# LayerNorm's small product on GpSimd, one more graph's rows by TensorE, and a new plan, in a two-layer graph attention kernel

## The chip, the core and the metric

The kernel runs on one core of a Trainium2 chip. The core has five engines with their own instruction streams: TensorE (PE in the profile; PEld is its weight load), VectorE (DVE), ScalarE (ACT), GpSimd (POOL) and SyncE (SP), which here only issues DMAs. Each engine takes its instructions strictly in the order in which they were written; they meet through semaphores. The metric is device time in microseconds, from the first instruction to the last with what lies around them.

## What is computed

There are 32 graphs of 512 nodes with 512 features in f32. Two layers, each with a LayerNorm, a ReLU and a residual:

```python
h = relu(layernorm(x));  x = x + L0(h, adj)
h = relu(layernorm(x));  x = x + L1(adj, h, W1, ..., W2, ...)

# L0: one head, on the features themselves
s = leaky_relu((h @ w_src)[:, :, None] + (h @ w_dst)[:, None, :] + b, 0.2)
attn = softmax(where(adj + eye == 0, -inf, s), axis=-1);  out = attn @ h

# L1: a layer of 4 heads with 256 features each (W1), ELU, a layer of 1 head (W2)
xl = x @ W;  e = leaky_relu(asrc[:, :, None] + adst[:, None, :], 0.2)
attn = softmax(where(mask, e, -1e9), axis=1);  out = attn^T @ xl + bias
```

## The kernel before

The body does not run a loop on the chip: all instructions of all 32 graphs are written out. The nodes of a graph are four tiles of 128 partitions. Each step is recorded with `op(engines, cost, emit, reads, writes, ...)`, where a cost is a pair or more of nanoseconds: how long the engine is occupied, how long after that the result is there, and for a DMA how long the transfer holds the DMA engines. `Plan.run` then makes one draft (`DRAFTS = 1`): a list scheduler in Python which, on the host and before anything runs, plays the program on five engines with these costs and writes the instructions out in the order that comes out. Of the steps that are ready, an engine takes the one with the lowest rank. The rank is the TensorE work recorded ahead of the step, less 1000 times the number that `LEADS` gives for the step's stage and engine (`"S0:DVE"`, `"first C:SP"`): a larger lead means earlier. The draft also decides which place a buffer gets. On the chip nothing of its times remains but each engine's order and each buffer's place; the instructions wait for data, not for times.

Two more of its rules matter. A step with `lock=True` on VectorE or GpSimd is not begun, in the draft, while a locked step of the other runs. And `self.turns` makes buffers of a kind be taken in the order in which they are first used, so the second graph's `x` cannot be loaded before the first's.

The stages of a graph, by the names that `LEADS` uses: LX loads x; S0 is the first LayerNorm, the ReLU, eight dot products with `ws_r` and `wd_r` on VectorE (line 464, VectorE's) and the scalar added to them (line 990); M0 loads and prepares the first mask; g (`guards`) computes a bound per row for the exponent, with line 796; e (`edge_weights`) makes the matrix of exponentials E: lines 840 (GpSimd), 845 (VectorE) and 852 (ScalarE), once for each of the four tiles. O0 is E times h on TensorE (line 864). I1 is the second LayerNorm, whose result is turned by DMA transposes (lines 701, 708, 717). P1 is the product with W1 (line 1178, a Strassen scheme with seven products). S10 to S13 and H0 to H3 are the four heads, P2 and O2 the last layer. O0 of graph b+1 and S0 of graph b+2 run inside the steps of graph b. For the first graphs this is not so: S0 and O0 of graph 0, I1 of graph 0 and S0 of graph 1 stand ahead of everything, and the stage name has "first " in front.

A vector of node values must be laid along the free dimension of all partitions for lines 796 and 845. There are two ways. `spread` does it on TensorE with four transposes of a broadcast column (line 634), straight into a PSUM bank. `in_lines` transposes once (line 748), copies to SBUF, writes to DRAM (line 754), and `row_of` reads it back to all partitions (line 765); `in_bank` copies it into PSUM (line 775). Before the change the first graph's layer-0 rows, and the last graph's rows of layer 2, go by `spread`, all others by `in_lines`. The guard's row goes by one of the same two ways (line 832 or 765).

LayerNorm (`layernorm`, from line 636): bn_stats and bn_aggr (lines 662 and 663), variance plus epsilon (line 665, VectorE), its power -1/2 on GpSimd (line 668), the negated product of mean and rstd on VectorE (line 673), and the ReLU with scale and bias on ScalarE (line 681). `STATS_BY_ACT` is False, so its other branch is not built.

The queues: SP issues every load of x, of the constants and of rows, the DMA transposes and the stores, in one order. GpSimd issues the adjacency loads (line 906), which turn int32 into bf16.

Of the kernel before, what the change touches and what calls it, by code (L numbers as in the profile page):

```python
# [13 lines left out]
ALU = mybir.AluOpType  # L14
# [29 lines left out]
class Plan:  # L44
# [8 lines left out]
        "first LXsoon:SP": 785.4, "first Csoon:SP": 105.6, "first C:SP": 575.5, "first Csoon:DVE": 111.1,  # L53
        "first Clater:DVE": -2168.5, "first Clater:SP": -124.3, "first S0:DVE": 54, "first S0:POOL": 54.1,
        "first S0:ACT": 54.2, "first S0M0:POOL": 40.3, "first S0M0:DVE": 37.9, "first S0M0:SP": 38,
        "first S0g:DVE": 220.7, "first S0g:PE": 221.7, "first S0e:PE": 116.5, "first S0e:ACT": 113.5,
        "first S0e:POOL": 117.7, "first S0e:DVE": 86.5, "first Clater:DVE+": -302.3, "first O0:PE": -14.2,
        "first O0:DVE": -14.9, "first Clater:PE": -622.9, "first I1:DVE": -27.8, "first I1:POOL": -32.7,
        "first I1:ACT": -34.4, "first I1:SP": 7.5, "first LX:SP": -173.2, "first S0:PE": 54.2, "first S0:ACT+": 54.8,
        "first S0:SP": 62.7, "first S0g:SP": 219.8, "first S0g:ACT": 226.9, "first S0g:ACT+": 259.3,  # L60
        "first S0e:SP": 132, "M1:POOL": -131.1, "M1:DVE": -58.6, "M1:SP": 497.4, "P1:POOL": -271.5, "P1:DVE+": -315.5,
        "P1:PE": -560.7, "P1:ACT+": -104.3, "P1:DVE": 81.7, "S10:ACT+": 15.8, "S10:PE": -3.7, "S10:SP": -5.3,
        "S10g:DVE": 26.8, "S10g:SP": 355, "S10g:ACT": 151.7, "S10g:PE": -41.6, "S10g:ACT+": 196.8, "S10e:SP": 150.1,
        "S10e:ACT": 84.1, "S10e:POOL": -13.9, "S10e:DVE": -29.6, "S11e:SP": 370.2, "S11e:ACT": -6.8,
        "S11e:POOL": -831.1, "S11e:DVE": -7.7, "O0:PE": -520.4, "O0:DVE": 9.8, "I1:DVE": -434.5, "I1:POOL": -437.7,
        "I1:ACT": -353.3, "I1:SP": -45.6, "LX:SP": 182.7, "S12:ACT+": -353.7, "S12:PE": -47.7, "S12:SP": 0.5,
        "S12g:DVE": -41.3, "S12g:SP": 287.8, "S12g:ACT": 166.3, "S12g:PE": -55.7, "S12g:ACT+": -10.5,
        "S12e:SP": 191.8, "S12e:ACT": -11.3, "S12e:POOL": 0, "S12e:DVE": 20.5, "H0:PE": -147.3, "H0:DVE": -16.3,
        "H0:ACT": -2, "H0:SP": 0, "S13e:SP": 153.5, "S13e:ACT": 138, "S13e:POOL": -420.2, "S13e:DVE": -145.4,
        "H1:PE": -1610.5, "H1:DVE": 44.9, "H1:ACT": 38.6, "H1:SP": -31.7, "H2:PE": -576, "H2:DVE": 407.8,  # L70
        "H2:ACT": 670.6, "H2:SP": 3.2, "H3:PE": 316.5, "H3:DVE": 329.5, "H3:ACT": 324.6, "H3:ACT+": 322.5,
        "S0:DVE": 48.1, "S0:POOL": -92, "S0:ACT": 170.3, "S0M0:POOL": -90, "S0M0:DVE": 97.6, "S0M0:SP": 153.4,
        "S0:PE": 282.3, "S0:ACT+": 102.1, "S0:SP": 553.1, "S0g:DVE": -202.3, "S0g:SP": 242.1, "S0g:ACT": 78.5,
        "S0g:PE": -64.8, "S0g:ACT+": 99.9, "S0e:SP": 151.7, "S0e:ACT": 344.9, "S0e:POOL": -14.4, "S0e:DVE": 19.6,
        "P2:POOL": 58.8, "P2:DVE+": 280.5, "P2:PE": -75.7, "P2:ACT+": -435.8, "P2:DVE": 25.5, "P2:SP": 338.6,
        "P2g:DVE": 172.1, "P2g:SP": 311.2, "P2g:ACT": 10.2, "P2g:PE": -5.8, "P2g:ACT+": 428.5, "P2e:SP": 238.7,
        "P2e:ACT": -58.2, "P2e:POOL": 63.9, "P2e:DVE": 117.7, "LB:SP": -2.9, "O2:PE": -586.8, "O2:DVE": 16.2,
        "O2:SP": 60.8, "last M1:POOL": 0.9, "last M1:DVE": -1.5, "last M1:SP": 22.2, "last P1:POOL": -254.4,
        "last P1:DVE+": 31.5, "last P1:PE": -56.6, "last P1:ACT+": -28.8, "last P1:DVE": -133.8,
        "last P2:POOL": -56.3, "last P2:DVE+": 1.4, "last P2:PE": 73.3, "last P2:ACT+": -39.5, "last P2:DVE": 13.5,  # L80
        "last P2:SP": -19.7, "last P2g:DVE": 147.5, "last P2g:SP": 95.3, "last P2g:ACT": 124.4, "last P2g:PE": 164.3,
        "last P2g:ACT+": 22.4, "last P2e:SP": 266.3, "last P2e:ACT": 228.3, "last P2e:POOL": 239.4,
        "last P2e:DVE": 228.3, "last S10:ACT+": 75.4, "last S10:PE": 27.1, "last S10:SP": 53.7, "last S10g:DVE": 71.7,
        "last S10g:SP": 27.3, "last S10g:ACT": 65.5, "last S10g:PE": 117, "last S10g:ACT+": 88.3, "last S10e:SP": 267,
        "last S10e:ACT": 276.6, "last S10e:POOL": 256.6, "last S10e:DVE": 253.5, "last S11e:SP": -323.5,
        "last S11e:ACT": -369.7, "last S11e:POOL": -375.4, "last S11e:DVE": -374.6, "last S12:ACT+": -443.3,
        "last S12:PE": -467.6, "last S12:SP": -468, "last S12g:DVE": -49.5, "last S12g:SP": -48.7,
        "last S12g:ACT": -62.1, "last S12g:PE": -46.6, "last S12g:ACT+": -85.4, "last S12e:SP": -67.5,
# [253 lines left out]
def kernel(  # L342
# [1015 lines left out]
    if B > 1:  # L1358
        load_x(1)
        layer0_scores(1)  # L1360
# [56 lines left out]
```

## Time and profile before

| quantity | value |
|---|---|
| median of 3 runs | 3603.31 us (3600.66 to 3608.34) |
| the profiled execution | 3606.86 us, its span 3604.9 us |
| granted TensorE clock, mean | 0.991 |
| VectorE busy | 2896.2 us (80%) |
| ScalarE busy | 1999.0 us (55%) |
| GpSimd busy | 1464.9 us (41%) |
| DMA traffic | 446.14 MB, mean 124 GB/s |
| chain of work that ended last | PE 76%, DVE 10%, DMA 7%, ACT 4% |

The profile is of one execution. Busy time of an engine is the sum over its instructions; the records of a matmul overlap their neighbours, so TensorE's busy time says that it had work in hand, not that it ran at its best. The chain of waits is followed back from the last instruction: what released it, what released that, and so on.

### The profile page before, as it was taken

To read this page: it belongs to the slowest core of one execution; us is meant where nothing else is said; L and a number is where in the kernel's file an instruction comes from. 1 tells how busy PE (TensorE), PEld (TensorE's weight loads), DVE (VectorE), ACT (ScalarE), POOL (GpSimd) and SP (SyncE) were. 2 spreads that over 40 slices of the span, in tenths; PEclk is the share of its full clock that TensorE was granted. 3 is DMA by queue.
4 is the path that set the end of the run, shared out by engine and by line. 5 is a ranking of instruction groups with operands and counts; after the bars stand their busy time and mean duration, and the time that the engine had idled before them with its cause. 6 is when DMAs were issued, how large, how long until landed. Compare 5 with 4: busy or idle time off the path is not lost.

```text
span 3604.9 us, 49251 instructions
## 1 busy us (share of the span) xinstructions
PE 3446.4 (96%) x15924; PEld 2946.9 (82%) x15924; DVE 2896.2 (80%) x7650; ACT 1999.0 (55%) x3356; POOL 1464.9 (41%) x1352
## 2 busy tenths in 40 slices
PE   3999999999999999999999999999999999999999
PEld 2778888888888888888888888888888888888888
DVE  7887788877888877888788888778888788887765
ACT  2565556555565555565555655555655555655553
POOL 2444435434344434354343444443444343543442
PEclk8999999999999999999999999999999999999999
DMA  6344445445454454554554554544545545545532
GB/s 169 112 117 124 110 117 142 128 129 130 93 141 126 130 129 108 119 139 128 131 128 97 141 132 129 129 123 100 148 120 130 131 108 125 137 130 132 128 81 80
DMA packets 664995, 446.14 MB, mean 124 GB/s; under 512 B 486072, under 2 KB 525216, under 8 KB 664736
## 3 DMA queue, kind: packets, MB, share of 16 engines
q1 hardware_dynamic: 630944, 409.43, 42.5%
q0 software_dynamic: 33792, 33.56, 6.3%
q8 instruction: 126, 2.06, 0.2%
q14 instruction: 133, 1.09, 0.1%
HBM read 290.72 MB, written 68.28 MB: 100 GB/s over the span
## 4 chain that ended last, share of the span: by engine, by line
PE 76%; DVE 10%; DMA 7%; ACT 4%; issue 1%; POOL 1%; SPq 0%; ACTq 0%; DVEq 0%; POOLq 0%
PE acc L864 38%; PE acc L1178 37%; DVE junk L464 3%; DMA row<-lines 3%; DVE junk L796 2%; ACT big L717 2%; ACT big L681 1%; DMA x<-in_x_dram 1%; DMA lines<-flat 1%; DMA out_dram<-x 1%; DVE ac L990 1%; ACT row L701 1%; PE acc L634 1%; PE acc L748 1%; DVE st L662 1%
## 5 line engine op out<-in xcount | busy, mean ns | idle before, releaser
L864 PE MATMUL acc<-big,big 128*128 128x257 f32 (+1 forms) x8192 | 1976.5, 383 | 39.4 <-ACT big L852 26.0
L864 PEld LDWEIGHTS acc<-big,big 128*128 128x128 f32 x8192 | 1539.0, 191 | 296.0 <-ACT big L852 36.6
L840 POOL TENSOR_TENSOR big<-m,big 128x512 f32<-128x512 bf16 x768 | 924.5, 1221 | 711.8 <-DMA big<-lines 381.2
L852 ACT ACTIVATE big<-big,ac 128x512 f32<-128x512 f32 x768 | 542.2, 720 | 291.0 <-DVE big L845 289.1
L845 DVE SCALAR_TENSOR_TENSOR big<-acc,ac,big 128x512 f32<-128x512 f32 x768 | 552.8, 740 | 92.4 <-POOL big L840 63.2
L689 ACT COPY big<-acc 128x258 f32<-128x258 f32 (+2 forms) x581 | 219.7, 384 | 619.3 <-PE acc L1178 614.6
L796 DVE CUSTOM_DVE_ANT_0 junk<-m,acc 128x512 bf16<-128x512 bf16 x768 | 522.8, 681 | 37.0 <-ACT acc L775 25.1
L1178 PE MATMUL acc<-w,big 128*128 128x258 f32 (+1 forms) x2048 | 519.2, 380 | 0.0
L1178 PE MATMUL acc<-w_T,sum 128*128 128x258 f32 (+1 forms) x2048 | 504.9, 381 | 3.0 <-POOL sum L1059 2.0
L1178 PEld LDWEIGHTS acc<-w_T,sum 128*128 128x128 f32 x2048 | 386.6, 190 | 63.2 <-POOL sum L1059 2.8
L1178 PEld LDWEIGHTS acc<-w,big 128*128 128x128 f32 x2048 | 385.5, 189 | 55.4
L446 POOL MEMSET big<- 128x4 f32 (+1 forms) x128 | 13.6, 107 | 950.3 <-PE acc L864 812.0
L1261 ACT ACTIVATE v<-acc,minus_one 128x256 f32<-128x256 f32 x512 | 231.4, 470 | 254.2 <-DVE acc L1254 245.9
L882 DVE SCALAR_TENSOR_TENSOR x<-acc,r,x 128x256 f32<-128x256 f32 x512 | 242.9, 481 | 109.7 <-PE acc L864 102.4
L1189 DVE TENSOR_TENSOR big<-acc,big 128x258 f32<-128x258 f32 (+1 forms) x576 | 242.3, 421 | 90.4 <-PE acc L1178 88.2
L1178 PE MATMUL acc<-w_T,big 128*128 128x258 f32 (+1 forms) x1024 | 263.7, 380 | 0.0
L1178 PE MATMUL acc<-w_-T,big 128*128 128x258 f32 (+1 forms) x1024 | 258.8, 380 | 0.0
L1178 PE MATMUL acc<-w,sum 128*128 128x258 f32 (+1 forms) x1024 | 252.7, 380 | 0.0
L1254 DVE SCALAR_TENSOR_TENSOR acc<-acc,r,b_r 128x256 f32<-128x256 f32 x512 | 242.3, 484 | 4.8
L1265 DVE SCALAR_TENSOR_TENSOR v<-v,acc 128x256 f32<-128x256 f32 x512 | 200.5, 409 | 36.0 <-ACT v L1261 35.7
L717 ACT COPY big<-v 128x1024 uint16<-128x1024 uint16 x192 | 222.0, 1156 | 2.5 <-DMA v<-row 2.1
L1178 PEld LDWEIGHTS acc<-w,sum 128*128 128x128 f32 x1024 | 194.1, 190 | 28.2
(89 smaller groups left out, 3340.1 us busy)
## 6 DMA issues: line engine op xcount, KB each, us to landing
big<-lines SPq DMA_DIRECT2D x380, 256.0 KB
row<-lines SPq DMA_DIRECT2D x190, 256.0 KB
x<-in_x_dram SPq DMA_DIRECT2D x32, 1024.0 KB
m<-in_adj_dram POOLq DMA_DIRECT2D x64, 512.0 KB, 5.9
spill<-x SPq DMA_DIRECT2D x32, 1024.0 KB
x<-spill SPq DMA_DIRECT2D x32, 1024.0 KB
out_dram<-x SPq DMA_DIRECT2D x30, 1024.0 KB
v<-row SPq DMA_TRANSPOSE x192
```

What stands on the lines that cost most here:

```text
L689: "ACT": (on_act_copied(n), lambda: nc.scalar.copy(dst_of(), src_of())),
L717: nc.scalar.copy(out.bitcast(U16).rearrange("p k t (n b) -> p k t n b", b=2), values_of().bitcast(U16).rearrange("p (b t k n) -> p k t n b ...
L796: lambda t=t, j=j, a_row=a_row: nc.vector.tensor_tensor_reduce(by_blocks(junk), mask_row(mask_max, t), by_blocks(a_row.at), 1.0, LOWEST, A ...
L840: lambda t=t: nc.gpsimd.tensor_sub(by_blocks(E.at[:, t, :]), mask_row(mask, t), by_blocks(g_at())),
L845: lambda t=t: nc.vector.scalar_tensor_tensor(E.at[:, t, :], c_row.at, ac.at[:, 4 + j, t : t + 1], E.at[:, t, :], op0=ALU.max, op1=ALU.add),
L852: lambda t=t: nc.scalar.activation(E.at[:, t, :], E.at[:, t, :], AF.Exp, bias=ac.at[:, 2 * j, t : t + 1]),
L864: lambda s=s: nc.tensor.matmul(acc.at[:, :n], E.at[:, s, node_block(t)], of(s), start=(s == 0), stop=(s == T - 1)),
L882: lambda acc=acc, r=r, f=f, t=t: nc.vector.scalar_tensor_tensor(X.at[:, t, f], acc.at[:, :HD], r.at, X.at[:, t, f], op0=ALU.mult, op1=ALU. ...
L1178: lambda k=k: nc.tensor.matmul(acc.at[:, :width], at[a](k // 2)[:, k % 2, node_block(r)], weight_of(w, k, c), start=(begin and k == 0), st ...
L1189: op("DVE", on_dve(width), lambda: nc.vector.tensor_add(place(), acc.at[:, :width], place()), acc(0) + token, token)
L1254: lambda acc=acc, r=r: nc.vector.scalar_tensor_tensor(acc.at[:, :F], acc.at[:, :F], r.at, b1_r[:, h * F : (h + 1) * F], op0=ALU.mult, op1= ...
L1261: lambda i=i, v=v, acc=acc: nc.scalar.activation(v.at[:, i, :], acc.at[:, :F], AF.Exp, bias=minus_one), acc(0), v(i),
```

## The change

Four edits.

1. `layernorm`: VectorE negates the mean (a new step, 128x4), and GpSimd, which has just made rstd, multiplies the two itself. VectorE's product after GpSimd goes.
2. `layer0_scores`: the rows of graph 1, like those of graph 0, go by `spread` (`b > 1` in place of `b`; flag 3 stands for both rows).
3. Costs of the draft: constant loads, the occupation of SP by a transposed mask, and the step of line 990, which is also locked now. The two small VectorE steps of LayerNorm get 60 more elements as cost, and GpSimd's power 1050 in place of 1000 ns.
4. All of `LEADS` is new, and x and S0 of graph 1 have a stage of their own, "second ".

```diff
     LEADS = {
-        "first LXsoon:SP": 785.4, "first Csoon:SP": 105.6, "first C:SP": 575.5, "first Csoon:DVE": 111.1,
-        "first Clater:DVE": -2168.5, "first Clater:SP": -124.3, "first S0:DVE": 54, "first S0:POOL": 54.1,
...
+        "first LXsoon:SP": -70.5, "first Csoon:SP": -73.5, "first C:SP": -177, "first Csoon:DVE": -9.2,
+        "first Clater:DVE": -132.1, "first Clater:SP": -583.1, "first S0:DVE": -115.7, "first S0:POOL": -129.1,
...
+        "first I1:ACT": -316.8, "first I1:SP": -13.3, "second LX:SP": -31.3, "second S0:DVE": 237.4,
...
         def fetch(n, place, src, token, when):
-            op("SP", by_dma(4 * P * n), lambda: nc.sync.dma_start(place(), src), (), token, when)
+            op("SP", (600.0, 2500.0, 4 * P * n / 190.0), lambda: nc.sync.dma_start(place(), src), (), token, when)
...
-            op("DVE", on_dve(T), lambda: nc.vector.tensor_scalar(ve.at, mv.at[:, :, 1], EPS, None, op0=ALU.add), mv(*ROW), ve(0))
-            mean_of, sign = (lambda: mv.at[:, :, 0]), -1.0
-        op(
-            "POOL", (1000.0, 1000.0), lambda: nc.gpsimd.tensor_tensor(rstd.at, ve.at, minus_half, ALU.pow),
+            op("DVE", on_dve(T + 60), lambda: nc.vector.tensor_scalar(ve.at, mv.at[:, :, 1], EPS, None, op0=ALU.add), mv(*ROW), ve(0))
+            op(
+                "DVE", on_dve(T + 60), lambda: nc.vector.tensor_scalar(minus_mean.at, mv.at[:, :, 0], -1.0, None, op0=ALU.mult),
+                mv(*ROW), minus_mean(0),
+            )
+        op(
+            "POOL", (1050.0, 1080.0), lambda: nc.gpsimd.tensor_tensor(rstd.at, ve.at, minus_half, ALU.pow),
             ve(0), rstd(0), lock=True,
         )
         op(
-            "DVE", on_dve(T),
-            lambda: nc.vector.scalar_tensor_tensor(nmr.at, mean_of(), sign, rstd.at, op0=ALU.mult, op1=ALU.mult),
-            mean(*ROW) + rstd(0), nmr(0),
+            "POOL", (150.0, 200.0), lambda: nc.gpsimd.tensor_tensor(nmr.at, minus_mean.at, rstd.at, ALU.mult),
+            minus_mean(0, *((0, t) for t in ROW)) + rstd(0), nmr(0), lock=True,
         )
...
-                "SP", by_turning(2 * P * N * (T if whole else 1)),
+                "SP", (6500.0 if len(adj_loads) < 3 else 1800.0, *by_turning(2 * P * N * (T if whole else 1))[1:]),
...
-            "DVE", on_dve(T), lambda: nc.vector.tensor_scalar(ac.at[:, 1, :], ac.at[:, 1, :], b0_r, None, op0=ALU.add),
-            c + W["w0"]("rest"), c,
+            "DVE", on_dve(T + 60), lambda: nc.vector.tensor_scalar(ac.at[:, 1, :], ac.at[:, 1, :], b0_r, None, op0=ALU.add),
+            c + W["w0"]("rest"), c, lock=True,
...
-        lines = in_lines(first(ac, 2), scores, 2) if b else None
-        L0[b] = (h0, edge_weights(scores, ac, lines, 0, guards(scores, ac, lines, 1, m0, 0 if b else 3), m0T))
+        lines = in_lines(first(ac, 2), scores, 2) if b > 1 else None
+        L0[b] = (h0, edge_weights(scores, ac, lines, 0, guards(scores, ac, lines, 1, m0, 0 if b > 1 else 3), m0T))
...
     if B > 1:
+        plan.stage = "second "
         load_x(1)
         layer0_scores(1)
+        plan.stage = "first "
```

## The prediction

> **What bounds the kernel now.** I read the page first, then the table by stretches, then TensorE's waits, then the order of instructions around the two largest.
>
> ```profile
> PE 3446.4 (96%) x15924; PEld 2946.9 (82%) x15924; DVE 2896.2 (80%) x7650; ACT 1999.0 (55%) x3356; POOL 1464.9 (41%) x1352
> PE   3999999999999999999999999999999999999999
> ```
>
> TensorE is busy 3446.4 of 3604.9 us; 158.5 us are open to a better order. The forty digits show one poor slice, the first. The table by stretches (PE busy second after the length; the column behind POOL is the granted clock) says how the 158.5 divide:
>
> ```profile
> 0.00:105.00 105.00, 44.28 (x157) 34.93 (x158) 77.22 (x253) 25.86 (x33) 21.94 (x29) 0.84 0.61 150
> 105.00:420.00 315.00, 296.14 (x1350) 251.47 (x1349) 259.13 (x708) 187.62 (x317) 136.34 (x124) 0.98 0.46 119
> 420.00:3300.00 2880.00, 2807.65 (x13023) 2403.01 (x13022) 2347.93 (x6131) 1630.08 (x2746) 1198.66 (x1102) 1.00 0.50 125
> 3300.00:3604.00 304.00, 298.36 (x1398) 257.49 (x1397) 211.95 (x561) 155.45 (x261) 107.94 (x99) 1.00 0.40 106
> ```
>
> Idle: 60.7 us up to the first graph's P1 (line 1178 begins at 105), 18.9 in the next 315, 72.4 in the even stretch (26 graphs of some 110 us, so 2.75 us each), 5.6 at the end. TensorE's waits name the causes:
>
> ```profile
> PE acc L748 <- DVE ac L990: 52.8, 28, 2.4
> PE acc L634 <- DVE junk L464: 30.6, 4, 27.1
> PE acc L864 <- ACT big L852: 26.0, 5, 11.7
> PE acc L748 <- DVE guard L814: 22.0, 13, 9.4
> ```
>
> So there are two places: the start (rows two and three, and 9.4 of row four) and one repeated wait of 52.8/28 = 1.89 us per graph.
>
> **The start, before.** Timeline of the three steps that hold it:
>
> ```profile
> 25.53 0.69 DVE L464 SCALAR_TENSOR_TENSOR junk<-big,ws_r 128x512 bf16<-128x512 f32 x1
> ...
> 62.88 0.27 PE L748 MATMUL acc<-ident,ac 128*8 128x128 f32 x1 [1.84 <-DVE x L882]
> ...
> 84.46 4.89 POOL L840 TENSOR_TENSOR big<-m,big 128x512 f32<-128x512 bf16 x4 [12.56 <-DMA big<-lines]
> ```
>
> Graph 0's x has landed at 6.32 (bn_stats starts) and its ReLU runs 11.33 to 14.26, but the dots begin at 25.53: `ws_r` was issued at 12.80, behind the attention vectors and W1, and was scaled at 23.85. The dots end at 31.91, E's first tile reaches TensorE at 47.21 (15.3 us later), O0 of graph 0 ends at 67.1. From there to P1 there are 38 us: bn_stats, the product on VectorE (L673 at 75.22, though GpSimd's power was done at 71.9: four L796 stood ahead of it), the ReLU, transposes, sums. Graph 1's x was issued at 30.56; its dots end at 62.21, and its E reaches TensorE at 88.44.
>
> **Part 1, order of loads.** The new ranks on SP put x of graph 0 first, then x of graph 1 (its lead -31.3 and some 22 us of recorded work give about 53, but it must wait its turn), then `ws_r`, `wd_r`, `b0_r` (73.5), and only then the vectors and W1 (177). At 300 GB/s (the DMA rate of 5 to 10 us), 1 MB of x and 0.5 MB of the two vectors are 5 us behind x of graph 0: landed about 12. Dots can begin at 12.5 in place of 25.5, 13 us earlier. All is not gained. "second S0:DVE" leads by 237.4, so graph 1's bn_stats (4 x 0.66, with aggregation 3.5) and dots (8 x 0.73 = 5.9) may go ahead of graph 0's: that is up to 9.4 us back. Bounds on graph 0's E: 13 and 3.6 us earlier; I take 8. W1 then lands some 5 us later than its 12.9 to 22, but nothing on TensorE needs it before P1. SP is held 5.83 us by the first transposed mask (issued 22.42); x of graph 1 and the vectors are past it now, only W1's remainder and the later constants stand behind.
>
> **Part 2, graph 1 by TensorE.** It removes two `in_lines` and three `row_of`: five DMAs. By the trace: end of L990 62.44 to the row in its bank 68.47 (row landed 67.88, ScalarE copy 0.59) = 6.0 us; graph 0 by `spread` takes from 32.14 to 33.05 = 0.9. Guard ready 76.31 to GpSimd's start 84.46 = 8.2; graph 0: 36.94 to 39.47 = 2.5. Together 10.8 us off graph 1's E. Twelve transposes of about 0.27 us (3.3 us) are added and two taken away; TensorE is empty there (3.94 us busy between 65 and 90), so they cost nothing; without that cover, 2.7 us. E of graph 1 arrives after x landed some 25 us earlier and this together well before 70.
>
> **Sum of the start.** What is late next is graph 0's path through O0 and I1 to P1. It moves by 8 us, and by the 3.3 us that L673 stood behind L796 at 75.22 (the product is now on GpSimd, not in VectorE's queue); O0 of graph 1 (17.1 us), which before filled the time from 88.44 to 105.55 and kept P1 from its data (the last L717 copy ends at 93.2), is done by then: up to 4 more. I take 14 us; bounds 3 and 25.
> The Trainium skill has a rule here ("TensorE: Matmul & The Clock Gate", why this matters for your kernels): avoid idle gaps over some 3 us, since the array falls back to half clock. The trace shows it: granted clock 0.50 from 75 to 90 and 0.55 from 90 to 95, so O0 of graph 1 lost about 3.5 us. The new start still has a gap before P1: by the rule a like loss stays, only on P1. By row and rule alike I book nothing back.
>
> **Part 3, LayerNorm.** 64 times. VectorE: one 128x4 step for another. L673 took a median 0.159 us and at most 1.234 (37.3 us over 53 in the even stretch); L665, the form of the new one, 0.16. If it escapes GpSimd it saves 53 x 0.54 = 29 us of VectorE, which has 19% to spare, so 0 on the time. GpSimd: the nearest rows are the memset of 128x4 (0.10 us) and the power of 128x4 (1.04); I take 0.15, nearer the memset since the power is the dear part: 64 x 0.15 = 10 us, bounds 6 and 66, on an engine idle 59%. Behind it in GpSimd's order stand L1059 and L840, whose readers would be 0.15 (at most 1.0) us later once in two LayerNorms' worth per graph. Nothing on TensorE in the even stretch waits for L673 or L681 by name. I book 0; from -5 to +10 us.
>
> **Part 4, the repeated wait.** One graph's order around it:
>
> ```profile
> 797.28 7.21 POOL L840 TENSOR_TENSOR big<-m,big 128x512 f32<-128x512 bf16 x5 [4.90 <-DMA big<-lines]
> ...
> 798.08 1.46 DVE L464 SCALAR_TENSOR_TENSOR junk<-big,ws_r 128x512 bf16<-128x512 f32 x1
> ...
> 799.59 1.52 DVE L464 SCALAR_TENSOR_TENSOR junk<-big,wd_r 128x512 bf16<-128x512 f32 x1
> ...
> 801.04 1.11 DVE L990 TENSOR_SCALAR ac<-ac,b_r 128x4 f32<-128x4 f32 x1
> ...
> 802.21 0.27 PE L748 MATMUL acc<-ident,ac 128*8 128x128 f32 x1 [2.40 <-DVE ac L990]
> ```
>
> Two dots take 1.46 and 1.52 in place of 0.69, and L990 1.11 in place of its free 0.22: all three lie beside GpSimd's L840. Behind the waiting transpose stand 62 matmuls, so each microsecond is TensorE's. The plan expected L990 to cost 0.07. The slip is 0.89 from L990 and 1.6 from the dots. The change prices L990 at 0.14 and keeps it, in the draft, off GpSimd. If the plan so places the transpose later by L990's excess, 28 x 0.89 = 25 us go.
> Against this speaks the skill's page "SBUF — State Buffer" (who interferes with whom): VectorE and GpSimd share a port pair as an exclusive lock, and whichever starts first keeps it for its whole instruction. A lock in a host's draft holds no engine: it works only where GpSimd really starts when the draft says. The dots were locked in the old draft too, and still were doubled. By L990's row the gain is 25 us, by this reading 0. I take half, 12; bounds -53 (the wait gone wholly) and 0.
>
> **Part 5, the rest of the plan.** Every lead is new, so every order in the even stretch is. No row shows what that does. TensorE's 2.75 idle us per graph bound the gain (72 us with part 4 in it). For the loss the nearest row is the wait above: one more transpose or matmul set 1.9 us too early, in each graph. I take 0. The end has 5.6 us idle in 304: -4 to +10, taken 0.
>
> **Sum.** -14 - 12 = -26 on the profiled 3606.9: 3581. This execution lay 3.6 us above the median of the runs, so **3577**.
>
> **Rivals.**
> - **The wait goes wholly.** The new order puts in_lines behind enough matmuls: -53 - 15 = -68, 3535. For it: the costs mended (L990, L673) are those that the trace shows mispriced. Against: the 1.6 us from the dots, which the prices do not touch.
> - **Nothing is left.** 14 us from the start, given back at 0.5 us per graph in the even stretch: 3603.
> - **A new wait per graph.** A transpose (L748) or product set too early behind a VectorE or GpSimd step that slips: 28 x 1.9 = +53, less 14: 3642. It decides from 0.5 us per graph on. For it: VectorE is 82% busy, a slip repeats in each graph since all graphs have one order, and L814 already makes such waits (22.0 us, 13 times). Against: the wait of L990 stands there already and the new prices are closer.
> - **The start does not move** because graph 1 ahead on VectorE eats it: 3591, inside the first case's range.
>
> **Chances.** The forecast 0.46 (its own range 3555 to 3596), wait gone 0.19, nothing left 0.09, a new wait 0.26. What can be told from no change is 0.2%, 7 us: faster 0.65, same 0.09, slower 0.26. The range runs from 3527 to 3630: it leaves out the deep end of the second case (0.04) and the larger half of the last (0.15).
>
> **What would show it.** Right: `ws_r` issued before 5 us and the first dots near 12 to 16; no line 748 or 754 before 100 us; P1's first matmul near 91 in place of 105; L990 near 0.2 us and its wait under 30 us in TensorE's list. Wrong: P1 later than 102; a wait with 28 entries under another name; L990 still at 1.1. GpSimd's new step over 0.5 us would move its 10 us to over 30. If TensorE's idle time between 420 and 3300 exceeds 86 us, the last rival has won.

## The result, and the profile after

The changed kernel takes 3590.05 us (median of 18 runs, 3585.65 to 3596.36); the kernel before, run beside it on the same chip, 3603.84 us (18 runs). The ratio is 0.9964, with a 95% interval of 0.9956 to 0.9972: 13.8 us faster where 26 were forecast. The direction was right, the size half.

Lines of the changed kernel are one higher than before from line 464 on, LayerNorm's own apart (464 is 465, 748 is 749, 990 is 991, 1178 is 1179); the new product of LayerNorm on GpSimd is line 674.

First the table by stretches of the changed kernel, with the columns and the stretches shown before:

```profile
0.00:105.00 105.00, 55.47 (x234) 46.68 (x235) 89.35 (x286) 37.97 (x52) 31.47 (x37) 0.90 0.67 153
105.00:420.00 315.00, 291.77 (x1319) 246.92 (x1318) 253.83 (x695) 176.84 (x296) 134.29 (x126) 0.96 0.46 117
420.00:3300.00 2880.00, 2813.79 (x13053) 2410.92 (x13052) 2332.47 (x6220) 1626.43 (x2679) 1218.66 (x1162) 1.00 0.51 126
```

TensorE's idle time in the first 105 us fell from 60.7 to 49.5 us, in the even stretch from 72.4 to 66.2, and rose from 18.9 to 23.2 between 105 and 420. Then TensorE's waits:

```profile
PE acc L749 <- DVE ac L991: 57.8, 29, 2.3
PE acc L635 <- DVE ac L991: 22.0, 1, 22.0
PE acc L865 <- ACT big L853: 15.3, 6, 11.1
```

The repeated wait, 52.8 us in 28 before, stands there as it was. The guard's wait under the transpose of line 748 (22.0 us in 13 before) is gone; at the start, where two graphs go by `spread` now, two single waits on guard steps stand under line 635 (10.3 and 9.3 us).

When did each kernel have the same share of TensorE's matmul records behind it? Worked out from the starts in both traces:

```
share of matmuls        1%     2%     3%     4%     5%    10%    40%    95%   99.9%
before, us            105.6  147.0  183.4  225.9  260.3  438.8 1500.7 3431.6 3597.2
after, us              77.5  123.0  162.2  219.1  253.7  428.9 1485.3 3416.2 3584.5
lead of the change     28.1   24.0   21.2    6.8    6.6    9.9   15.3   15.4   12.7
```

So the start won over 20 us, 14 of them were lost again in one place, the even stretch won about 9, the end lost 3. The place is seen in the stretch that holds the same 160 matmuls in each kernel, first before, then after:

```profile
183.00:226.00 43.00, 35.68 (x163) 30.32 (x163) 39.45 (x120) 25.74 (x43) 15.81 (x15) 0.92 0.47 117
```

```profile
162.00:219.00 57.00, 39.62 (x162) 30.98 (x161) 47.06 (x135) 28.86 (x45) 16.53 (x15) 0.85 0.43 93
```

57 us in place of 43, at a clock of 0.85 in place of 0.92. (From 3% to 4% of the matmuls it is 55 to 60 us in all fourteen later runs that keep the changed kernel's plan, so this is no chance of one execution.) Its largest wait is the first exponents of graph 2 (line 853), 11.1 us at 198.6, where the kernel before waited 7.3.

### The profile page after: what moved, and what is told of

Its sections match the earlier page's. It is cut to its first block, busy times and chain, and to the rows that moved or that the text cites. A ratio compares the mean times of both kernels' runs of the same rounds, so it can differ in the third digit from the quotient of the medians.

```text
span 3592.2 us, 49368 instructions
## 1 busy us (share of the span) xinstructions
PE 3445.8 (96%) x15934; PEld 2949.1 (82%) x15934; DVE 2877.7 (80%) x7726; ACT 1990.1 (55%) x3274; POOL 1488.4 (41%) x1419
## 4 chain that ended last, share of the span: by engine, by line
PE 79%; DVE 7%; DMA 6%; ACT 6%; issue 1%; POOL 0%; SPq 0%; ACTq 0%; DVEq 0%; POOLq 0%
PE acc L1179 40%; PE acc L865 37%; DVE junk L465 3%; DMA row<-lines 3%; ACT big L718 2%; ACT big L682 2%; DVE junk L797 2%; DMA v<-row 2%; DMA lines<-flat 1%; ACT row L702 1%; DVE ac L991 1%; PE acc L635 1%; PE acc L749 1%; DMA big<-lines 1%; ACT big L853 0%
## 5 line engine op out<-in xcount | busy, mean ns | idle before, releaser
L841 POOL TENSOR_TENSOR big<-m,big 128x512 f32<-128x512 bf16 x768 | 927.3, 1225 | 642.2 <-DMA big<-lines 357.7
L853 ACT ACTIVATE big<-big,ac 128x512 f32<-128x512 f32 x768 | 540.9, 720 | 217.0 <-DVE big L846 214.7
L690 ACT COPY big<-acc 128x258 f32<-128x258 f32 (+2 forms) x526 | 203.1, 387 | 746.9 <-PE acc L1179 721.3
L846 DVE SCALAR_TENSOR_TENSOR big<-acc,ac,big 128x512 f32<-128x512 f32 x768 | 551.6, 740 | 63.8 <-POOL big L841 52.1
L1060 POOL TENSOR_TENSOR sum<-big,big 128x512 f32<-128x512 f32 x31 | 39.0, 1260 | 466.3 <-ACT big L718 466.3
```

Source lines behind the costliest of these rows:

```text
L690: "ACT": (on_act_copied(n), lambda: nc.scalar.copy(dst_of(), src_of())),
L841: lambda t=t: nc.gpsimd.tensor_sub(by_blocks(E.at[:, t, :]), mask_row(mask, t), by_blocks(g_at())),
L846: lambda t=t: nc.vector.scalar_tensor_tensor(E.at[:, t, :], c_row.at, ac.at[:, 4 + j, t : t + 1], E.at[:, t, :], op0=ALU.max, op1=ALU.add),
L853: lambda t=t: nc.scalar.activation(E.at[:, t, :], E.at[:, t, :], AF.Exp, bias=ac.at[:, 2 * j, t : t + 1]),
```

## The experiments

Sixteen kernels were run, each beside the kernel before on the same chip. A planner that is asked anew may draw a whole new order, so most of them keep every engine's order and every buffer's place of the changed kernel and alter one thing; the two that are planned anew are marked. The kernel before lay at 3601 to 3605 us (medians) in these sessions, so a few us against the changed kernel's 3590 mean nothing. The diffs of those that move steps show the order of instructions on an engine.

### The repeated wait: first try

The first two take the place apart: the transpose set later, and the addition of line 991 on another engine.

```diff
 the S0 transpose of line 749, its copy and its DMA write, in the order of the draft
-start[i]
+start[i] + 2100.0
```

> The changed kernel's order kept, except that in S0 the transpose of line 749, its copy and its DMA to DRAM stand 2.1 us (some five matmuls) further back in their engines' orders. Theory A (TensorE is the bound and this wait is lost time, 57.8 us in 29 graphs): the wait under 10 us, the time 40 to 55 us lower, about 3540. Theory B (the wait is slack: the next step is late by the same amount, so another wait takes its place): the wait of line 749 gone, others up by as much, the time within 7 us of the changed kernel.

Measured: 3592.65 us, ratio 0.9975 [0.9965, 0.9985]: nothing gained. The wait on line 991 went, and an equal one came (lines here are 17 higher than in the changed kernel, so 882 is 865 and 708 is 691):

```profile
PE acc L882 <- DVE flat L708: 54.6, 30, 2.5
```

The matmul behind the moved transpose needs the PSUM bank that the transpose fills and VectorE's copy must empty first.

```diff
-nc.vector.tensor_scalar(ac.at[:, 1, :], ac.at[:, 1, :], b0_r, None, op0=ALU.add)
+nc.scalar.activation(ac.at[:, 1, :], ac.at[:, 1, :], AF.Identity, bias=b0_r)
```

> The changed kernel's order kept; the scalar of line 991 is added by ScalarE in place of VectorE, at the same place of the order. Theory A (line 991 takes 1.11 us only because GpSimd's line 841 runs beside it on what the two share; ScalarE does not share it): the step 0.2 to 0.3 us, the wait of line 749 shorter by 0.7 to 0.9 us per graph, 20 to 26 us off the time. Theory B (the two dots ahead are the delay, and a wait on another engine adds what is saved): under 8 us.

Measured: 3553.22 us, ratio 0.9866 [0.9850, 0.9882], 37 us under the changed kernel. On ScalarE the addition takes 0.30 us and is done before the last dot, so it leaves the path; what is left is the last dot:

```profile
PE acc L749 <- DVE r L1252: 30.0, 28, 1.5
```

That is 57.8 - 30.0 = 27.8 us less waiting. The rest of the 37 is clock, told at the end: 3.4 us at half clock between 420 and 3300 in place of 23.9, so some 10 us.

### LayerNorm, and VectorE's total

```diff
-"POOL", (150.0, 200.0), lambda: nc.gpsimd.tensor_tensor(nmr.at, minus_mean.at, rstd.at, ALU.mult)
+"POOL", (150.0, 200.0), lambda: nc.vector.tensor_tensor(nmr.at, minus_mean.at, rstd.at, ALU.mult)
```

> The changed kernel's order kept; LayerNorm's small product is made by VectorE again (the negated mean stays a step of its own), at the same place of the order. Theory A (the product is on no path that TensorE waits for, from I1 and S0 of the even graphs): within 7 us of the changed kernel. Theory B (GpSimd's own product is what the change gained): slower by 8 to 14 us, mostly in the first 260 us.

Measured: 3591.26 us, ratio 0.9972 [0.9962, 0.9981], no different from the changed kernel. On GpSimd line 674 takes a median of 0.216 us (at most 0.713), on VectorE 0.155 (at most 1.012). ScalarE's ReLU waits for the VectorE form 76.9 us in 33 entries, and TensorE notices none of it.

The next leaves out the 32 dots that VectorE makes for W2's score columns at the start (these columns are set to 0). It asks whether VectorE's sheer work there makes the hole at 170 to 200 us.

```diff
-dot(lo[:, 2:], flat(att[1])[:, i * D : i * D + W2 - 2], part[:, k, i : i + 1])
+nc.vector.memset(lo[:, i : i + 1], 0.0)
```

> The changed kernel's order kept, but the 32 dot products on VectorE that make the two score columns of W2 are left out (the columns are set to 0), some 16 us of VectorE in the first 105 us. Theory A (VectorE's work holds the first 200 us, and that is where the 21 to 28 us of lead at 80 to 180 us go): P1 of graph 0 begins at 82 as before or earlier, the hole of TensorE between 170 and 200 us shrinks, 8 to 16 us off the time. Theory B (that hole is the chain of DMAs and row loads of graph 1's first head): under 3 us off.

Measured: 3589.01 us, ratio 0.9969 [0.9956, 0.9981], and the wait for graph 2's first exponents is still 11.6 us, though VectorE is busy 80.60 us of the first 105 in place of 89.35. The total does not make the hole.

### The repeated wait: moving it about

```diff
 TensorE, in each graph
-L749 (S0's scores)
 L865 x5
+L749 (S0's scores)
```

> The changed kernel; every engine's order and every place kept, except that on TensorE up to five matmuls that stood behind the S0 transpose of line 749 now stand ahead of it (some 1.3 us and more of work). Theory A (the wait on line 991 is an order on TensorE alone: a transpose some 2 us too early, with other matmuls behind it that have their data): the wait on L991 falls from 57.8 us to under 15, TensorE idles 40 to 55 us less than in the changed kernel, the half-clock windows that follow the waits go too (up to 10 us), and the time is 3530 to 3550. Theory B (what stands behind is no readier, or it needs the transpose's PSUM bank, as in the run with the transpose postponed): an equal wait turns up under another name and the time stays within 10 us of 3590.

> Both edits together: line 991's addition on ScalarE (3553 alone) and up to four matmuls ahead of the S0 transpose of line 749. What is left of the wait with the addition on ScalarE is 30.0 us in 28 entries, 1.07 each, on the last dot. Theory A: it goes too, 20 to 28 us, so 3525 to 3533. Theory B: the matmuls put ahead leave the transpose's chain (transpose, copy, line write, row load, guard) too late for the exponents of that graph, and a wait on L853 or L814 takes its place: no faster than 3548.

Measured: 3593.39 us, ratio 0.9963 [0.9951, 0.9975], and with the addition on ScalarE 3554.66, ratio 0.9858 [0.9844, 0.9871]. Neither moves by more than 4 us from the kernel that it was made from. The first kernel's waits:

```profile
PE acc L865 <- ACT big L853: 65.5, 33, 11.5
```

The transpose no longer waits, and the matmuls behind it wait for exponents instead, about as long. Both stand behind the same dots in VectorE's queue: the transpose behind line 991, and L853 behind an L846 that VectorE reaches 2 us after it. Theory B held in each, with VectorE's queue as the thing behind it. The next two therefore move L846 forward too.

```diff
 VectorE, in each graph, on top of the last two
 L465 ws_r (tile 4)
+L846
 L465 wd_r (tile 4)
+L846
 L1252, L1255, L691, L1266 ...
-L846
-L846
```

> The version of 3555 (line 991 on ScalarE, up to four matmuls ahead of the S0 transpose) with two more moves in each graph: on VectorE the next two L846 stand on either side of S0's last dot instead of some 2 us behind it, and on ScalarE the first of their L853 stands ahead of three L1262. Theory A (what TensorE lacks at this place is VectorE's queue: the doubled dots delay whatever stands behind them, first the transpose, and when that is out of the way L846 and with it L853): the wait on L853, 50.0 us in 34, loses its 28 or so entries of 1.2 us, and the time is 3520 to 3532. Theory B (the chain behind S0's scores to the next layer-0 exponents is what binds, and it is as long as before): the wait turns up elsewhere and the time stays within 6 us of 3555.

> The same two moves on the version with line 991 left on VectorE and up to five matmuls ahead of the transpose (3593). There L853 is waited for 65.5 us in 33 entries, some 1.8 each. Theory A (VectorE's queue): with L846 in front, most of that goes, line 991 at its 1.1 us notwithstanding; what is left is the transpose, for which five matmuls are not cover enough by about 0.7 us: 3545 to 3565. Theory B (line 991 and its late transpose bind by themselves): above 3580.

Measured: with the addition on ScalarE 3553.39 us, ratio 0.9856 [0.9843, 0.9870], nothing gained; with it on VectorE 3565.63, ratio 0.9891 [0.9876, 0.9906], 28 us gained, just past the slow end of what theory A expected. In the first the long waits went (TensorE's idle time in the even stretch fell from 43.7 to 16.6 us), and yet no time was gained: the steps between two matmul starts show many small hold-ups instead, 283 of 0.235 to 0.6 us with 42 us over the usual 0.217, where there had been 52 with 6. TensorE's busy time hides them. What each of them waits for was not followed; it looks as if, whatever stands first in VectorE's queue, something behind it is late.

### The repeated wait: its cause

If VectorE's queue is it, then a microsecond taken from it anywhere ahead of the place must count, and line 991 can stay as it is. The next kernel halves four of the eight dots (scores of the first two tiles over 256 of 512 features, from graph 2 on).

```diff
-dot(h0.at[:, t, :D], w, ac.at[:, i, t : t + 1])
+n = D // 2 if b > 1 and t < 2 else D
+dot(h0.at[:, t, :n], w[:, :n], ac.at[:, i, t : t + 1])
```

> The changed kernel with every order kept; from the third graph on, the S0 dots of the first two tiles run over 256 of the 512 features (scores differ for these nodes): four steps of 0.42 us in place of 0.69, 1.1 us less on VectorE per graph, as much as line 991 takes, and ahead of it. Line 991 is left alone. Theory A (any microsecond taken from VectorE's queue at this place counts, whichever step gives it): the wait on L991 falls by about 1 us a graph, from 57.8 to under 35, and the time by 25 to 40, as with the addition on ScalarE: 3550 to 3565. Theory B (line 991's own collision with GpSimd sets the wait, and GpSimd's L841 starts when its row lands): dots that end sooner only lengthen nothing, line 991 still takes 1.1 and the wait stays over 45 us: above 3580.

Measured: 3520.28 us, ratio 0.9770 [0.9756, 0.9783]. Taking 1.1 us per graph gave 70 us, 2.3 per graph, and the wait on line 991 fell from 57.8 to 4.2 us. More came back than was taken out, since the dots now mostly end before GpSimd's L841 begins: of the last 28 graphs, all had dots of over 1 us in the changed kernel, and 10 have here.

```profile
PE acc L749 <- DVE ac L991: 4.2, 11, 1.0
```

So it was looked for where VectorE could save the time with nothing left out. Here is the place in the changed kernel, in the timeline of VectorE, of GpSimd, of SP and of TensorE:

```profile
785.14 0.43 DVE L691 COPY big<-acc 128x257 f32<-128x257 f32 x1 [1.25 <-PE acc L1179]
785.48 0.27 DVE L691 COPY flat<-acc 8x128 f32<-8x128 f32 x1
...
786.01 0.69 DVE L465 SCALAR_TENSOR_TENSOR junk<-big,ws_r 128x512 bf16<-128x512 f32 x1
...
790.62 1.46 DVE L465 SCALAR_TENSOR_TENSOR junk<-big,ws_r 128x512 bf16<-128x512 f32 x1
792.12 1.52 DVE L465 SCALAR_TENSOR_TENSOR junk<-big,wd_r 128x512 bf16<-128x512 f32 x1
793.58 1.11 DVE L991 TENSOR_SCALAR ac<-ac,b_r 128x4 f32<-128x4 f32 x1
```

```profile
790.16 5.74 POOL L841 TENSOR_TENSOR big<-m,big 128x512 f32<-128x512 bf16 x4 [4.89 <-DMA big<-lines]
```

```profile
785.77 0.30 SPq L755 DMA_DIRECT2D lines<-flat  x1
787.05 0.36 SPq L766 DMA_DIRECT2D big<-lines  x1
```

```profile
794.74 0.27 PE L749 MATMUL acc<-ident,ac 128*8 128x128 f32 x1 [2.05 <-DVE ac L991]
```

VectorE stands idle for 1.25 us behind a copy that waits for TensorE (the bracket of the first row), with all eight dots queued behind it, though the first tile has been ready since 784.7. At 790.16 its row releases GpSimd's L841; the last two dots run beside it, and each takes twice its time. The row has its origin in the same place: it is the guard's line, which the second copy (`flat`, 785.48) takes out of PSUM, and which SP then writes to DRAM (L755) and reads back (L766). The next kernel moves two dots, on VectorE alone:

```diff
 VectorE, in each graph
+L465 ws_r (tile 1)
+L465 wd_r (tile 1)
 L691, L691, L691, L784
-L465 ws_r (tile 1)
-L465 wd_r (tile 1)
 L465 ws_r (tile 2) ...
```

> The changed kernel; on VectorE alone, in each graph, the first two S0 dots (first tile, whose ReLU is done at 784.7 in the graph looked at) stand ahead of three copies of line 691 and line 784; the first copy waits for TensorE until 785.14, with VectorE idle for 1.25 us. Nothing is left out. Theory A (any microsecond of VectorE's queue ahead of the transpose counts): the dots end about 1.2 us sooner, most of them before GpSimd's L841 begins, the wait on L991 falls from 57.8 us to under 25, the half-clock windows go, and the time is 3520 to 3550. Theory B (the copies, now 1 us later, are wanted as urgently: the heads' scores go through them): a wait on L749 or L865 behind L691 of 1 us a graph takes its place, and the time is above 3575.

> The same order on VectorE, with line 991's addition on ScalarE (3553 alone, where 30.0 us in 28 entries are left on the last dot). Theory A: that wait goes too, and the time is 3515 to 3528, a few us under the run with line 991 on VectorE. Theory B: as for the other, above 3545.

Measured: 3526.42 us (3524.2 to 3529.6), ratio 0.9788 [0.9775, 0.9802], and with line 991 on ScalarE as well 3526.27, ratio 0.9785 [0.9771, 0.9798]. Two dots moved by four steps are worth 64 us, and the addition's engine is worth nothing any more. The same place in the first of the two:

```profile
771.80 0.69 DVE L465 SCALAR_TENSOR_TENSOR junk<-big,ws_r 128x512 bf16<-128x512 f32 x1 [0.83 <-ACT big L682]
...
773.49 0.27 DVE L691 COPY flat<-acc 8x128 f32<-8x128 f32 x1
...
777.81 0.69 DVE L465 SCALAR_TENSOR_TENSOR junk<-big,wd_r 128x512 bf16<-128x512 f32 x1
778.42 1.12 DVE L991 TENSOR_SCALAR ac<-ac,b_r 128x4 f32<-128x4 f32 x1
```

```profile
778.35 4.65 POOL L841 TENSOR_TENSOR big<-m,big 128x512 f32<-128x512 bf16 x4 [6.01 <-DMA big<-lines]
```

```profile
780.13 0.27 PE L749 MATMUL acc<-ident,ac 128*8 128x128 f32 x1
```

All dots take 0.69 us and end as L841 begins. Line 991 still takes 1.12, and nothing waits for it: the transpose has no bracket. In TensorE's list 1.0 us is left on line 991. A wait of the kind that theory B named has come, 0.36 us per graph where it said 1, and the even stretch is nearly full:

```profile
PE acc L749 <- DVE ac L691: 10.8, 30, 1.9
PE acc L749 <- DVE ac L991: 1.0, 1, 1.0
```

```profile
420.00:3300.00 2880.00, 2860.27 (x13341) 2461.89 (x13340) 2344.58 (x6380) 1670.51 (x2752) 1218.53 (x1187) 1.00 0.53 129
```

This version beats both kernels, by 77 and 64 us: 50 of the 64 are TensorE's idle time (146.4 us in the changed kernel, 96.3 here, each the span less PE's busy time), and some 12 the clock in the even stretch.

Why did the collision end? The 1.25 us that VectorE stood idle are not the reason. They shrink only to 0.83, in which it now waits for the first tile's ReLU. And in the run with five matmuls ahead of the transpose (3593) there is a graph in which VectorE does not idle at this place at all (the copy has no bracket), and the last two dots are doubled all the same:

```profile
788.55 0.43 DVE L691 COPY big<-acc 128x257 f32<-128x257 f32 x1
...
794.08 1.46 DVE L465 SCALAR_TENSOR_TENSOR junk<-big,ws_r 128x512 bf16<-128x512 f32 x1
...
795.58 1.53 DVE L465 SCALAR_TENSOR_TENSOR junk<-big,wd_r 128x512 bf16<-128x512 f32 x1
```

What counts is the order of the dots and the `flat` copy. Worked out from the traces for the last 28 graphs, L841 begins 4.4 to 5.5 us after the end of that copy in the changed kernel (median 4.4) and 4.4 to 5.1 us after it here (4.6): a copy that comes later starts GpSimd later. With eight whole dots behind the copy, the last ends 1.7 to 3.6 us after L841 has begun, in every graph; with six, from 0.4 before it to 0.4 after, and none is doubled. The kernel before has the same order here, and in all of its last 28 graphs the last dots are doubled too.

The move of the two dots thus did two things. Two dots fewer lie between the copy and L841; and the copy itself comes 0.9 us later behind the guard (it begins a median 2.5 us after the end of L815 in place of 1.6), and L841 with it. The run with half dots did the first alone: its copy stayed at 1.6 us, the dots behind it were 1.1 us shorter, and 18 of the 28 graphs became free of doubled dots. The second was not tried alone.

### Prices and leads (both planned anew)

```diff
-"DVE", on_dve(T + 60), lambda: nc.vector.tensor_scalar(ac.at[:, 1, :], ...), c + W["w0"]("rest"), c, lock=True
+"DVE", on_dve(T), lambda: nc.vector.tensor_scalar(ac.at[:, 1, :], ...), c + W["w0"]("rest"), c
```

> The changed kernel, but line 991 priced and unlocked as before; planned anew, so every order may differ. Theory A (a lock and 0.07 us more in a draft hold no engine): L991 still takes about 1.1 us, the wait on it is still about 2 us in 28 or 29 entries, and the time is within what a new order scatters, some 10 us of 3590 either way. Theory B (price and lock did part of the work, something else in the new order undid it): L991's wait grows to over 3 us in each graph or the time by over 25 us.

```diff
 the kernel before
-LEADS = {"first LXsoon:SP": 785.4, ...}
+LEADS = {"first LXsoon:SP": -70.5, ...}
+plan.stage = "second "
 load_x(1)
 layer0_scores(1)
+plan.stage = "first "
```

> The kernel before with the new leads and the stage of its own for graph 1's x and S0, and nothing else: LayerNorm's product, graph 1's rows, all prices as before; planned anew. Theory A (leads and prices belong together, and a plan with either alone is a new draw): over 20 us slower or faster than 3590, with a wait of some 28 entries that neither kernel has. Theory B (the leads carry the gain by themselves): 3580 to 3600.

Measured: 3727.2 us, ratio 1.0327 [1.0309, 1.0344], without the price and lock of line 991; 3828.03, ratio 1.0621 [1.0606, 1.0635], with the leads alone. Of the first, theory A's reading of line 991 held (median 1.11 us, 29 waits of 2.08), and its guess that the time stays within 10 us did not: its time, 137 us up, is what theory B said, though line 991's own wait did not grow. Of the second, theory A held in its time, and in its list L853 stands first with 67.5 us in 28. The waits of the first:

```profile
PE acc L865 <- DVE r L877: 84.1, 28, 3.8
PE acc L749 <- DVE ac L991: 60.4, 29, 3.4
```

A new wait of 3.0 us per graph stands first, exactly of the kind that the prediction's last rival described. The price and lock of one 128x4 step hold nothing on the chip, but they are part of the input from which the planner draws all orders, and in these two plans the leads did not fit other prices than those with which they were made. A difference between two plans says nothing about the step whose price was changed.

### The start

In the changed kernel graph 0's dots end at 21.6 us in place of 31.9, yet the first product of O0 begins at 47.21 in both. TensorE's timeline shows who stands in front:

```profile
46.30 1.12 PE L635 MATMUL acc<-ident,guard 128*128 128x128 f32 x4 [10.28 <-DVE guard L815]
47.21 29.04 PE L865 MATMUL acc<-big,big 128*128 128x257 f32 x128
```

These four are graph 1's guard, ahead of graph 0's O0 in TensorE's order. Two kernels give graph 0 its way within the first 60 us, the second further than the first:

```diff
 VectorE
+L804, L815 (graph 0)
 L465 x8, L991 (graph 1)
+L846 x4 (graph 0)
-L804, ..., L815 (graph 0)
 sums over the weights, mask and guard steps of graph 1
-L846 x4 (graph 0)
 TensorE
+L635 x4 (guard of graph 0)
 L635 x8 (scores of graph 1)
-L635 x4 (guard of graph 0)
 the second kernel also: graph 1's mask and guard steps ahead of the sums (VectorE), and
-L635 x4 (guard of graph 1)
 L865 (graph 0, 16 products)
+L635 x4 (guard of graph 1)
```

> The changed kernel; order on VectorE and TensorE altered only within the first 55 us: lines 804 and 815 of graph 0 stand ahead of graph 1's eight dots, its four L846 right behind them, and its guard's four transposes ahead of graph 1's. Theory A (the 13 us that the loads gained for graph 0 were eaten by graph 1's dots and later steps standing first on VectorE): E of graph 0 reaches TensorE at 35 to 37 us in place of 47.2, line 1179 begins up to 10 us earlier, and the time is 5 to 10 us under the changed kernel's. Theory B (the start's lead is given back later whatever its size, as 14 us of it were between 162 and 219 us): E and line 1179 come earlier by as much, but the time stays within 3 us. If E does not come before 44 us, something else held it and A falls.

> The changed kernel; only the first 60 us re-ordered, further than in the last such run: on VectorE graph 0's guard steps, graph 1's dots, graph 0's four L846, graph 1's mask and guard steps, and only then the sums over the weights; on TensorE the first 16 products of O0 of graph 0 stand ahead of graph 1's guard transposes; on ScalarE all L853 of graph 0 ahead of graph 1's row copy. Theory A (O0 of graph 0 was held at 47.2 by graph 1's guard transposes in front of it in TensorE's queue, and by VectorE's order): first L865 at 37 to 40 us, line 1179 at 71 to 76, and 5 to 9 us off the whole, 3581 to 3586. Theory B (a lead of the start is given back at 160 to 220 us): line 1179 as early, but the time within 2 us of 3590.

Measured: 3593.31 us, ratio 0.9962 [0.9948, 0.9977], and 3591.65, ratio 0.9963 [0.9951, 0.9976]; no gain. In the first O0 still stood behind graph 1's guard, now at 50.84. In the second it began at 38.04, 9 us earlier, and the product with W1 went on in earnest at 93.86, not earlier than the changed kernel's 90.94. There theory A's first half held and its second did not. VectorE's queue explains it in part: by the time P1 runs in earnest, it has been busy 77.28 of the first 91 us in the changed kernel, 77.22 of the first 105 before. That is its work ahead of P1, and re-ordering it saves none. A test of that takes VectorE's dots away from it for a while, by the load order alone:

```diff
 SP
 x of graph 0, x of graph 1
-ws_r, wd_r, b_r
 the attention vectors, W1
+ws_r, wd_r, b_r
```

> The changed kernel; only SP's order of the first loads altered: ws_r, wd_r and the scalar are issued behind the attention vectors and W1 again (with what hangs on it moved on VectorE: two mask steps come ahead of the vectors' scaling). Theory A (VectorE has some 77 us of work ahead of the first product with W1 in earnest, and is busy 77 of the first 91 us, so each microsecond by which its dots begin later is lost): dots begin at 22 to 26 in place of 14.6, line 1179 goes on in earnest at 97 to 101 in place of 91, and the time is 5 to 10 us above 3590. Theory B (the load order is worth nothing, since graph 0's E waits for graph 1's guard anyway): P1 within 2 us of 91 and the time within 2 us of 3590.

Measured: 3603.43 us (21 runs), ratio 0.9999 [0.9991, 1.0007]: the whole gain of the change is gone with three loads. VectorE stands idle 10.52 us for `ws_r`, and P1 goes on in earnest at 102.11, 11.2 us late:

```profile
26.21 0.43 DVE L496 TENSOR_SCALAR ws_r<-ws_r 128x512 f32<-128x512 f32 x1 [10.52 <-DMA ws_r<-in_L_gnn_attn_w_src_dram]
```

VectorE's work is not the whole of it, though. In the run without W2's dots it was busy only 73.91 of the first 91 us, and P1 went on in earnest at 90.45, 0.5 us earlier. The sum that P1 needs (line 1058 there) waited for ScalarE's copy of the transposes:

```profile
89.70 0.69 DVE L1058 TENSOR_TENSOR sum<-big 128x512 f32<-128x512 f32 x1 [2.70 <-ACT big L717]
```

So graph 0's own path (O0, LayerNorm, transposes) ends close behind VectorE's other work. The late loads put off both (O0 begins at 58.17 there in place of 47.21), so that run shows what the load order is worth, not which of the two holds P1.

The shift also tells something of the 14 us lost between 162 and 219 us. At equal counts of matmuls the three kernels of this section lie 4.4, 3.4 and 11.2 us behind the changed one at 3% and 4.5, 3.6 and 11.3 at 4%, and 5.0, 3.8 and 11.0 at the end. A lag of up to 11 us thus passes through that place whole, so nothing fixed in time holds it; it is a hole that the changed kernel's order has, and the old order has less of. No run reached it with a larger lead. What in that order makes it was not settled: the chain of waits there runs over VectorE's dots for two graphs in a row, a row load into a buffer that is freed by a head's last products, the guard's line and its row. The graphs share buffers and banks there, and no run takes these apart.

## Why the prediction was right and wrong

**Part 1, load order: right in size, by another way.** `ws_r` was issued at 1.80 us and the dots began at 14.62, within the 12 to 16 foretold; 13 us were worked out, and the run that takes the order back costs 13. I then took off 5 for graph 1's priority. That step was wrong: graph 1 did eat the 13 us of graph 0's E, all of them (47.21 in both kernels, outside the bounds of 3.6 and 13), but the product with W1 waits for the end of VectorE's whole work, in which it does not matter whose dots come first, and close behind it for the transposes.

**Part 2 and the sum of the start.** P1's first matmul was foretold near 91; eight early ones stand at 81.71 and 83.72, and P1 goes on in earnest at 90.94. Its 14 us were too few there (24 at 2% of the matmuls) and too many in the end, where 6.6 were left at 5%: I followed the lead to P1 and not to the next place where an order can lose it. What the rows by TensorE alone are worth was not tried: it cannot be taken back without a new plan. Of the 3.3 us that I booked for taking LayerNorm's product out of VectorE's queue nothing was found: with the product back on VectorE the same share of matmuls (2%) is reached at 123.1 us as without.

**The rule on idle gaps.** I booked no clock gain at the start. The granted clock of the first 105 us rose from 0.84 to 0.90, but in the hole behind it fell from 0.92 to 0.85. The first of these varies: the runs of 3592.65, 3593.39 and 3520.28 us show 0.97 with hardly another order there.

**Part 3, LayerNorm: right.** Booked at 0, and no difference could be told. GpSimd's step took 0.216 us where 0.15 was taken, 14 us of its time in 64 where 10 were counted.

**Part 4, the repeated wait: wrong.** "By L990's row the gain is 25 us, by this reading 0. I take half, 12": it was 0, the wait even 5 us longer. The reading by the Trainium skill's "SBUF — State Buffer" (who interferes with whom) was the right one, with L991 at 1.11 us as before, and the half was an average of two mechanisms of which only one can be. The row of L990 was misread in a second way. I counted 0.89 us of slip for it and 1.6 for the dots as separate faults with separate cures. They are one fault: all eight dots stand behind the copy whose line releases L841 some 4.4 us later, so the last dots and line 991 run into it. Two dots moved ahead of that copy take the wait from 57.8 us to 1.0, with line 991 at its 1.12 us.

**Part 5 and the end.** Taken as 0; the even stretch gained about 9, mostly the guard's wait (10.1 us of it, in 10, lay between 420 and 3300), and the end lost 3. The range for the end was -4 to +10.

**The sum.** -14 and -12 were forecast; 7 came from the start, 0 from the wait, 9 from the even stretch, and 3 were lost at the end. The failed steps are two terms. Part 4's 12 us took a price and a lock in the host's draft to shorten the wait on line 990; it stayed (57.8 us after 52.8), because the order that makes it, all eight dots behind the guard's copy, is the same in both kernels. The start's 14 were counted at P1; half of them, 6.6, were left at 5% of the matmuls. That the total reached half the forecast owes 9 us to the even stretch, for which nothing was booked: luck.

**The rivals.** Nothing in the changed kernel shows a new wait per graph, but two plans that were drawn with part of the edits have one (84.1 and 67.5 us, in 28 each), so the 0.26 was not idle. "The wait goes wholly" would have needed the order of two dots, not a price.

## What to carry to other kernels

When an engine's wait repeats in each iteration, do not stop at the step named by it, nor at the engine that waits: read the named engine's own queue, and ask what starts the engine beside which its steps slow down. Here one copy in VectorE's queue did both: ready dots stood behind it, and its line started GpSimd. Moving the waiter only renamed the wait; moving two ready dots in front of that copy cured it, and gave back more than their own length because it ended a collision. An idle gap next to a slow step need not be its cause: look for an iteration that has the one without the other. In a planned kernel, test an edit with every order frozen, since a new plan moves the time by more than most edits do.

## What the runs showed of the hardware

**A gap of 2 us can halve TensorE's clock for 3.4 us.** In the even stretch the trace's clock record shows windows of 3.4 us at half clock (6.8 where two follow each other). Over the traces of both kernels and the sixteen runs, between 420 and 3300 us, there are 123. Each begins within 1.6 us of the end of a gap between two matmul starts. Gaps counted by what they have over the usual 0.217 us:

```
gap                 how many     followed by a half-clock window
0.9 to 1.6 us          205          0
1.6 to 2.5 us          313         97
over 2.5 us             36         26
```

The Trainium skill ("TensorE: Matmul & The Clock Gate", why this matters for your kernels), weighed in the prediction, puts the limit at gaps of some 3 us; here 2 us were enough in nearly a third of the cases, and the measurement decides. So the same wait is hit in one graph and spared in the next. A window costs some 1.7 us (an estimate: half of 3.4). The changed kernel had 7 of them in the even stretch, the run with the addition on ScalarE 1, the two with two dots moved none, and the one without price and lock 32, 147 us at half clock that cost about 73: nearly as much as its new wait.

**VectorE and GpSimd.** A dot of 128x512 takes 0.69 us and 1.46 to 1.52 beside L841, the 128x4 addition 0.21 and 1.11. On ScalarE the addition took 0.30 in all 32 graphs, in 28 of them beside L841.
